# State-space stage: the scan, the segment product and the scaled C are written over the decay tile they are made from, in a pool of three such tiles

## The chip, the cores and the metric

One core of one Trainium2 chip runs the whole kernel as one program. The core's engines work side by side, each with its own stream of instructions: PE (TensorE, matrix products and transposes), DVE (VectorE), ACT (ScalarE), POOL (GpSimd), and SP (SyncE), which here does little but issue DMA transfers. The metric is the device time of one execution in microseconds (us). It was taken in three runs of the kernel before, and once more in an execution recorded by the profiler.

## The reference

A small stack of layers on `x` with 1024 tokens of width 512, all float32:

```python
x = x + 0.5 * _L0_ffn_ref(_layernorm(x), ...)    # 8 experts, mean of the top 2
x = x + _L0_attn_ref(_layernorm(x), ...)         # causal attention, 32 heads
x = x + 0.5 * _L0_ffn_ref(_layernorm(x), ...)    # the same experts again
x = x + 0.5 * _L1_ffn_ref(_layernorm(x), ...)    # dense layer + LoRA experts
x = x + _L1_attn_ref(_layernorm(x), ...)         # state-space layer
x = x + 0.5 * _L1_ffn_ref(_layernorm(x), ...)
```

The change is in the state-space layer. A projection of the normalized `x` gives a gate, an input `x`, a B and a C for each of 8 groups, and a step size `dt` for each of 64 heads; B, C and `x` go through a causal convolution over four tokens and a SiLU. Each group has eight heads of 64 channels with a state of 64 x 128 per head. Then:

```python
dt_p = softplus(dt + dt_bias)
dA = exp(dt_p * -exp(A_log))
dtx = dt_p[..., None] * x
def step(state, inp):
    dA_t, dtx_t, B_t, C_t = inp
    state = state * dA_t[..., None, None] + dtx_t[..., None] * B_t[:, :, None, :]
    y_t = einsum('bhpn,bhn->bhp', state, C_t)
    return state, y_t
y = ys + x * D
yn = y * rsqrt(mean(y * y over the group) + EPS) * norm_weight * silu(gate)
out = einsum('bli,di->bld', yn, out_proj_w)
```

The kernel doesn't step through tokens. For a chunk of 128 tokens and one head, the part of `y` that comes from within the chunk is a product with a 128 x 128 matrix: entry (s, l) is the product of B of token s with C of token l, times the decay from s to l, and 0 where s comes after l. The part that comes from earlier chunks is the state at the chunk's start times C, scaled by the decay from the chunk's start to token l.

## The kernel before, in words

The layers ahead of it (experts, attention, experts, LoRA layer) are not touched. The state-space stage is the function `mamba`. It starts by computing, for all tokens and heads, the step sizes and the decays. The decays of each token (`da`) and those accumulated since the chunk's start (`ecum`) are written to a scratch tensor `decay` in DRAM, in two halves of 512 tokens (the DMA that ends that stretch of code).

Then come 8 groups `g`, each in two halves `hf` of 512 tokens: 16 units of four chunks `i`, 64 chunks in all. In the prediction a chunk is named by its `i` in the unit or by its number 0 to 63. One group of two units needs four weight loads, all from the queue of SP and into a pool of four buffers: `w_bc`, `w_x`, `w_g`, and last `w_out`, which ACT scales (L1044). Each chunk has three parts.

`prepare(un, i)` makes the operands:

- SP issues two DMAs that bring the chunk's decays and accumulated decays of eight heads (1024 floats each) from DRAM, copied to all 128 partitions, into the two halves of a tile `dd` (L1157; 512 KB each).
- DVE runs a scan along the first half, with a unit matrix `eye8` as the addend, and so makes the decays from s to l into a tile `e` (L1163); it then multiplies `e`, in place, with the product `gt` of B and C (L1171).
- PE transposes the convolved `x` (`ps_tr`), DVE multiplies it with the step sizes: `xdt` (L1176). GpSimd makes `xw` of it (L1182) for the next state.
- GpSimd multiplies C with the second half of `dd` into a tile `cs` (L1188; not for the first chunk of a group, which has no state before it).

`scan(un, i, ...)` does the chunk: PE multiplies `xdt` with `e` and the state with `cs`, both into `ps_y` (L1206); DVE adds the skip term (`y_m`, L1215); ACT squares it (`sq`, L1219); DVE multiplies it with the gate (`yg`, L1221); PE makes the chunk's addition to the state (`ps_st`, L1224); GpSimd scales the old state (L1231), DVE adds (L1234); GpSimd sums the squares in two steps (L1236 on 256 columns, L1237 on 128).

`project_out` has PE sum the squares over the partitions (`ps_ss`, L1243), DVE turn that into a normalizing factor `ss` (L149, L150), PE multiply `yg` with `w_out` (`ps_out`, L1250), and DVE scale it and add it to `x` (L1253).

Between these, the next unit's projections are made in slices, two in chunk 0 and one in each of the other three: `ps_in` on PE (L227); the convolution on ACT (L1055) and DVE (L1059, and L1068 for the first columns of a second half, which read the last columns of the first half from `hist`; L1077 writes these); the SiLU on ACT (L1078).

The order in which the program writes this down in chunk `i` is: `scan(i)`, the projection slices for the next unit (at `i == 1` also the transposes and product `gt` of the next unit's B and C), `prepare(i + 1)`, `project_out(i)`. Each engine's own order is then laid down by the framework's scheduler, which keeps to data and buffers: an operation goes no earlier than the buffers it needs can be free.

The tiles named above lie in a pool `m_e` (variable `ep`) of two buffers for each tag: `dd` with 8 KB in each partition, `e` and `cs` with 4 KB each. That makes 32 KB. `m_e` is the last pool opened in the stage.

The last group's units also run the first steps of the LoRA layer that follows (`after.step`), and the last unit has no next unit, so no projections lie between its chunks. The stage runs from about 1850 us of the span nearly to its end.

Of the kernel before, what the change touches and what calls it, by code (L numbers as in the profile page):

```python
# [13 lines left out]
F32 = mybir.dt.float32  # L14
# [8 lines left out]
P = 128  # L23
# [21 lines left out]
HPG = MH // MG  # L45
# [30 lines left out]
def macaron_kernel(  # L76
# [75 lines left out]
    def transposes(src, n):  # L152

        ps = psml.tile([P, 512], F32, tag="ps", name="ps_tr")
        for i in range(n):
            nc.tensor.transpose(ps[:, i * P : (i + 1) * P], src(i), ident)  # L156
        return ps
# [747 lines left out]
    def mamba(lora, par):  # L905
        conv, dsk, nwt, w_dt, dtb, av = par.conv, par.dsk, par.nwt, par.w_dt, par.dtb, par.av
        nct = MI // P
        with ExitStack() as ms:
# [13 lines left out]
            with tc.tile_pool(name="m_dt", bufs=1) as dp, tc.tile_pool(  # L922
                name="m_pair", bufs=3
# [97 lines left out]

            half = S // 2
            w2 = ms.enter_context(tc.tile_pool(name="m_w2", bufs=2))
            ep = ms.enter_context(tc.tile_pool(name="m_e", bufs=2))
            heads = [P, HPG, MP]

            def as_heads(a):
                return a.rearrange("p (h d) -> p h d", d=MP)
# [118 lines left out]
            def per_head(a, un, i):  # L1147
                c, h0 = 4 * un["hf"] + i, un["g"] * HPG
                return a[:, c, h0 : h0 + HPG].unsqueeze(2).to_broadcast(heads)

            def prepare(un, i):

                c, h0 = 4 * un["hf"] + i, un["g"] * HPG
                tok = slice(i * P, (i + 1) * P)
                dd = ep.tile([P, 2, HPG * P], F32, tag="dd", name="dd")
                for q in range(2):
                    nc.sync.dma_start(  # L1157
                        dd[:, q, :],
                        decay[un["hf"]][i, q, h0 * P : (h0 + HPG) * P].partition_broadcast(P),
                    )  # L1160

                e = ep.tile([P, HPG, P], F32, tag="e", name="e_seg")
                nc.vector.tensor_tensor_scan(  # L1163
                    e.rearrange("p h l -> p (h l)"),
                    dd[:, 0, :],
                    eye8.rearrange("p h l -> p (h l)"),
                    0.0,
                    ALU.mult,
                    ALU.add,
                )  # L1170
                nc.vector.tensor_tensor(  # L1171
                    e, e, un["gt"][:, i, :].unsqueeze(1).to_broadcast([P, HPG, P]), ALU.mult
                )
                ps = transposes(lambda k: un["xc"][:, k, tok], 4)
                xdt = w2.tile([P, D], F32, tag="xdt", name="xdt")
                nc.vector.tensor_tensor(  # L1176
                    as_heads(xdt), as_heads(ps), per_head(dtp, un, i), ALU.mult
                )
                xw = None
                if c < NCH - 1:  # L1180
                    xw = w2.tile([P, D], F32, tag="xw", name="xw")
                    nc.gpsimd.tensor_tensor(  # L1182
                        as_heads(xw), as_heads(xdt), per_head(erev, un, i), ALU.mult
                    )
                cs = None
                if c > 0:
                    cs = ep.tile([P, HPG, P], F32, tag="cs", name="cs")
                    nc.gpsimd.tensor_tensor(  # L1188
                        cs,
                        un["cT"][:, tok].unsqueeze(1).to_broadcast([P, HPG, P]),  # L1190
                        dd[:, 1, :].rearrange("p (h l) -> p h l", l=P),
                        ALU.mult,
                    )
                return e, xdt, xw, cs
# [66 lines left out]
            for j in range(5):  # L1261
                project_pair(un, j)
                if j == 1:
                    finish_bc(un)
            ready = prepare(un, 0)
            plan = ((0, 1), (2,), (3,), (4,))
            for n, _ in enumerate(units):
                nxt = None
                if n + 1 < len(units):
                    g, hf = units[n + 1]  # L1270
                    if hf == 0:
                        gr = load_group(g)
                    nxt = begin_unit(gr, hf)
                for i in range(4):
                    done = scan(un, i, *ready)
                    if nxt is not None:
                        for j in plan[i]:
                            project_pair(nxt, j)
                        if i == 1:
                            finish_bc(nxt)  # L1280
                    if i < 3:
                        ready = prepare(un, i + 1)
                    elif nxt is not None:
                        ready = prepare(nxt, 0)
                    project_out(*done)
                    if un["g"] == MG - 1:
                        after.step()
                        if nxt is None:
                            after.step(False)
                        elif i == 3:  # L1290
                            lora.load()
                            lora.store = True
                un = nxt
# [14 lines left out]
    with tc.tile_pool(name="lora", bufs=1) as lp:  # L1308
        lora, par = Lora(lp), Scan(lp)
        expert_ffn("f1", lambda: None, [lora.load, par.ready, par.turn], par.load)  # L1310
        mamba(lora, par)
# [51 lines left out]
```

## Time and profile before

| what | us |
| --- | --- |
| three runs of the kernel before, median | 3008.72 |
| lowest and highest of them | 3002.98, 3010.82 |
| the execution that the profiler recorded | 3011.75 |
| its span, first to last instruction | 3010.0 |

The mean TensorE clock granted over the span was 0.977 of full speed. The busy time of each engine by stretches of the span, in us:

| stretch | what runs | PE | DVE | ACT | POOL | clock |
| --- | --- | --- | --- | --- | --- | --- |
| 0 to 1850 | the layers ahead | 1713.73 | 894.93 | 401.58 | 266.62 | 0.88 to 1.00 |
| 1850 to 1950 | start of the state-space stage | 92.41 | 55.79 | 44.54 | 11.48 | 0.97 |
| 1950 to 2100 | groups | 149.38 | 110.79 | 40.00 | 74.04 | 1.00 |
| 2100 to 2300 | groups | 198.76 | 147.41 | 53.05 | 106.18 | 1.00 |
| 2300 to 2500 | groups | 198.99 | 148.08 | 56.37 | 101.93 | 1.00 |
| 2700 to 2900 | groups | 197.80 | 148.80 | 54.34 | 103.23 | 1.00 |
| 2900 to 3010 | last unit, end of the LoRA layer | 90.43 | 45.82 | 10.99 | 24.64 | 0.91 |

(The first row is the sum of the answers for 0 to 200, 200 to 900 and 900 to 1850 us, with their lowest and highest clock; the stretch from 2500 to 2700 is shown with the prediction.)

How the profile is read: a group of instructions has its engine, its line in the kernel, the operation, `output<-inputs` by the program's names, partitions x elements of output and input, and how often it occurs. Behind these stand the busy time and the mean time of one, then the engine's idle time just before, with what ended most of it ("the releaser"). In a timeline each row begins with its start and its duration in us, and the brackets at its end hold the idle time ahead of it and the releaser. The chain of waits is followed back from the last instruction, at each step to what released it. A busy PE is not PE at its peak, as its instructions' ends are modelled.

### The profile page before, as it was taken

What the parts mean: (1) busy time and instruction counts of PE and PEld (TensorE: products, weight loads), DVE (VectorE), ACT (ScalarE), POOL (GpSimd) and SP (SyncE); (2) the same over time, 40 slices, a digit from 0 to 9 for tenths busy, and PEclk for the clock granted to TensorE, in tenths of its full rate; (3) what the DMA queues carried; (4) which work ended last, traced back from release to release, by engine and by line L of the source; (5) the groups of instructions that cost most, each with busy time, mean ns of one, the idle gap of its engine ahead of it and who ended that gap; (6) DMA issues with size and microseconds to landing.
All of it is one profiled execution on the core that took longest, in us unless ns stands there. A gap on an engine that the chain in (4) does not pass through costs nothing.

```text
span 3010.0 us, 29285 instructions
## 1 busy us (share of the span) xinstructions
PE 2840.7 (94%) x10691; PEld 1525.9 (51%) x10691; DVE 1692.8 (56%) x3183; ACT 711.7 (24%) x1381; POOL 791.1 (26%) x601
## 2 busy tenths in 40 slices
PE   5979999999999999999999787999999999999988
PEld 3435646456564565655655344455555555455544
DVE  3146545465454654546445315677776777777673
ACT  1212212122121321213122121523222232222310
POOL 3231002020020200202000222144545545555451
PEclk8989999999999999999999898999999999999999
DMA  8420001010010100100002441232322322323210
GB/s 283 126 74 29 14 15 35 8 42 14 14 42 3 40 15 14 42 15 28 15 14 86 171 121 50 87 95 81 103 96 91 112 77 99 105 84 117 86 43 28
DMA packets 102174, 196.94 MB, mean 65 GB/s; under 512 B 9040, under 2 KB 34800, under 8 KB 102032
## 3 DMA queue, kind: packets, MB, share of 16 engines
q1 hardware_dynamic: 84896, 157.15, 15.8%
q0 software_dynamic: 6240, 20.45, 2.7%
q10 hardware_dynamic: 10896, 17.47, 1.6%
q8 instruction: 87, 1.43, 0.2%
q14 instruction: 55, 0.45, 0.1%
HBM read 176.17 MB, written 18.87 MB: 65 GB/s over the span
## 4 chain that ended last, share of the span: by engine, by line
PE 78%; DVE 12%; POOL 4%; issue 3%; DMA 2%; ACT 1%; POOLq 0%; DVEq 0%; SPq 0%; ACTq 0%
PE ps_in L227 14%; PE ps_m L823 13%; PE ps_o L728 8%; PE ps_wo L763 7%; PE ps_tr L156 6%; PE ps_out L1250 6%; PE ps_m L797 6%; PE ps_e L506 5%; PE ps_s L704 4%; DVE nm L715 3%; PE ps_y L1206 3%; PE ps_up L238 2%; DVE pr L720 1%; PE ps_st L1224 1%; DVE xc L1059 1%
## 5 line engine op out<-in xcount | busy, mean ns | idle before, releaser
L704 PE MATMUL ps_s<-kT,qT 128*128 128x512 f32 (+3 forms) x768 | 293.0, 491 | 1.8
L749 ACT COPY pT<-ps_tr 128x256 f32<-128x256 f32 (+2 forms) x192 | 91.9, 479 | 820.1 <-PE ps_tr L156 817.5
L728 PE MATMUL ps_o<-pT,v 128*128 128x512 f32 (+3 forms) x768 | 260.7, 489 | 0.0
L1250 PE MATMUL ps_out<-w_out,yg 128*128 128x512 f32 x512 | 240.7, 614 | 0.0
L227 PE MATMUL ps_in<-hT,w_g 128*128 128x512 f32 x512 | 227.1, 596 | 7.3 <-issue 7.3
L1188 POOL TENSOR_TENSOR cs<-cT,dd 128x1024 f32<-128x1024 f32 x56 | 183.5, 3278 | 162.6 <-PE ps_y L1206 140.4
L227 PE MATMUL ps_in<-hT,w_x 128*128 128x512 f32 x512 | 225.8, 593 | 0.0
L763 PE MATMUL ps_wo<-w_o,oT 128*128 128x512 f32 x512 | 222.0, 592 | 0.0
L718 ACT ACTIVATE pr<-ps_s,nm 128x128 f32<-128x128 f32 (+7 forms) x256 | 190.3, 743 | 132.5 <-DVE nm L715 107.8
L728 PEld LDWEIGHTS ps_o<-pT,v 128*128 128x128 f32 x768 | 146.4, 191 | 143.7 <-issue 107.2
L156 PE MATMUL ps_tr<-ident,pr 128*128 128x128 f32 x1152 | 172.9, 277 | 31.2 <-DVE sm L719 22.9
L632 POOL TENSOR_TENSOR sv<-w_v 128x512 f32<-128x512 f32 x7 | 8.9, 1269 | 723.3 <-PE ps_tr L156 466.9
L156 PEld LDWEIGHTS ps_tr<-ident,pr 128*128 128x128 f32 x1152 | 134.6, 142 | 115.3 <-issue 52.9
L715 DVE TENSOR_REDUCE nm<-ps_s 128x1 f32<-128x128 f32 (+7 forms) x256 | 189.4, 750 | 2.2
L506 PE MATMUL ps_e<-w_all,xt_s 128*128 (+1 forms) x368 | 168.8, 603 | 0.0
L227 PEld LDWEIGHTS ps_in<-hT,w_g 128*128 128x128 f32 x512 | 96.6, 190 | 126.9 <-issue 126.9
L227 PEld LDWEIGHTS ps_in<-hT,w_x 128*128 128x128 f32 x512 | 97.0, 190 | 121.0 <-issue 120.6
L1163 DVE TENSOR_TENSOR_SCAN e_seg<-dd,eye 128x1024 f32<-128x1024 f32 x64 | 152.3, 2380 | 7.8 <-PE ps_y L1206 6.8
L704 PEld LDWEIGHTS ps_s<-kT,qT 128*128 128x128 f32 x768 | 127.9, 193 | 54.8 <-issue 33.7
L763 PEld LDWEIGHTS ps_wo<-w_o,oT 128*128 128x128 f32 x512 | 96.2, 190 | 115.8 <-issue 115.8
L1059 DVE SCALAR_TENSOR_TENSOR xc<-ps_in,conv,xc 128x511 f32<-128x511 f32 (+2 forms) x192 | 141.6, 738 | 17.8 <-ACT xc L1055 17.4
L720 DVE TENSOR_SCALAR pr<-pr,sm 128x128 f32<-128x128 f32 (+7 forms) x256 | 145.8, 570 | 4.5
(252 smaller groups left out, 4416.8 us busy)
## 6 DMA issues: line engine op xcount, KB each, us to landing
dd<-decay SPq DMA_DIRECT2D x128, 512.0 KB
w_all<-in_w_e_dram SPq DMA_DIRECT2D x16, 1024.0 KB
outs<-y_e ACTq DMA_DIRECT2D x46, 256.0 KB
w_v<-in_wkv_dram SPq DMA_DIRECT2D x8, 1024.0 KB
w_q<-in_wq_dram SPq DMA_DIRECT2D x32, 256.0 KB
w_k<-in_wkv_dram SPq DMA_DIRECT2D x8, 1024.0 KB
w_o<-in_wo_dram SPq DMA_DIRECT2D x8, 1024.0 KB
w_x<-in_in_wt_dram SPq DMA_DIRECT2D x8, 1024.0 KB
```

Of the source, the lines that this page charges most:

```text
L156: nc.tensor.transpose(ps[:, i * P : (i + 1) * P], src(i), ident)
L227: nc.tensor.matmul(ps[:, cols : cols + n], lhsT=w[:, k, c0 : c0 + P], rhs=hT[:, k, t0 : t0 + n], start=(k == 0), stop=(k == KT - 1),)
L506: nc.tensor.matmul(ps, lhsT=xt[:, k, :], rhs=w_all[:, bass.ds(ep, 1), k, :].rearrange("p e c -> p (e c)"), start=(k == 0), stop=(k == KT - 1),
L704: nc.tensor.matmul(ps[:, j : j + m], lhsT=qT[:, qt * P : (qt + 1) * P], rhs=kT[:, j : j + m], start=True, stop=True,)
L715: nc.vector.tensor_reduce(nm, ps[:, :n], AX.X, ALU.max, negate=True)
L718: nc.scalar.activation(pr[:, :n], ps[:, :n], AF.Exp, bias=nm, accum_out=sm)
L728: nc.tensor.matmul(ps[:, lo:512], lhsT=v[:, kb, hh * P : (hh + 1) * P], rhs=pT[:, kb, lo:512], start=(kb == 0), stop=(kb == last),)
L763: nc.tensor.matmul(ps, lhsT=heads[hh][:, t * P : (t + 1) * P], rhs=w[:, hh, :], start=(hh == 0), stop=(hh == HG - 1),)
L797: nc.tensor.matmul(ps[:, t * 256 : (t + 1) * 256], lhsT=right[i][:, k, (j + t) * P : (j + t + 1) * P], rhs=left_v[i][:, k, :], start=(firs ...
L823: nc.tensor.matmul(ps, lhsT=gr["left"][i][:, k, hh * P : (hh + 1) * P], rhs=right[i][:, k, :], start=(first and k == 0), stop=(last and k ...
L1188: nc.gpsimd.tensor_tensor(cs, un["cT"][:, tok].unsqueeze(1).to_broadcast([P, HPG, P]), dd[:, 1, :].rearrange("p (h l) -> p h l", l=P), ALU ...
L1250: nc.tensor.matmul(po, lhsT=yg[:, k, :], rhs=w_o[:, k, :], start=(k == 0), stop=(k == 3))
```

## The change

The pool `m_e` gets three buffers instead of two, and only `dd` is left in it: 3 x 8 KB are 24 KB in each partition, where 2 x (8 + 4 + 4) were 32. The scan now writes `e` over the half of `dd` that it reads; the product with `gt` was in place on `e` before, and so is over `dd` as well. GpSimd writes `cs` over the other half of `dd`. No instruction is added or taken away, and no shape changes but for the way in which the tile is indexed. A tile `dd` is thus in use from its load until PE has read `e` and `cs` for `ps_y`.

```diff
--- before.py
+++ after.py
@@ -1021,7 +1021,7 @@
 
             half = S // 2
             w2 = ms.enter_context(tc.tile_pool(name="m_w2", bufs=2))
-            ep = ms.enter_context(tc.tile_pool(name="m_e", bufs=2))
+            ep = ms.enter_context(tc.tile_pool(name="m_e", bufs=3))
             heads = [P, HPG, MP]
 
             def as_heads(a):
@@ -1152,17 +1152,17 @@
 
                 c, h0 = 4 * un["hf"] + i, un["g"] * HPG
                 tok = slice(i * P, (i + 1) * P)
-                dd = ep.tile([P, 2, HPG * P], F32, tag="dd", name="dd")
+                dd = ep.tile([P, 2, HPG, P], F32, tag="dd", name="dd")
                 for q in range(2):
                     nc.sync.dma_start(
-                        dd[:, q, :],
+                        dd[:, q, :, :].rearrange("p h l -> p (h l)"),
                         decay[un["hf"]][i, q, h0 * P : (h0 + HPG) * P].partition_broadcast(P),
                     )
 
-                e = ep.tile([P, HPG, P], F32, tag="e", name="e_seg")
+                e = dd[:, 0, :, :]
                 nc.vector.tensor_tensor_scan(
                     e.rearrange("p h l -> p (h l)"),
-                    dd[:, 0, :],
+                    e.rearrange("p h l -> p (h l)"),
                     eye8.rearrange("p h l -> p (h l)"),
                     0.0,
                     ALU.mult,
@@ -1184,11 +1184,11 @@
                     )
                 cs = None
                 if c > 0:
-                    cs = ep.tile([P, HPG, P], F32, tag="cs", name="cs")
+                    cs = dd[:, 1, :, :]
                     nc.gpsimd.tensor_tensor(
                         cs,
                         un["cT"][:, tok].unsqueeze(1).to_broadcast([P, HPG, P]),
-                        dd[:, 1, :].rearrange("p (h l) -> p h l", l=P),
+                        cs,
                         ALU.mult,
                     )
                 return e, xdt, xw, cs
```

## Predicted, before the changed kernel was run

> **What bounds the kernel now.** I read the page's busy shares first, then busy time by stretches, then the chain of waits, and last the timeline of one group. The change touches the state-space stage alone, and there TensorE is full:
>
> ```profile
> PE 2840.7 (94%) x10691; PEld 1525.9 (51%) x10691; DVE 1692.8 (56%) x3183; ACT 711.7 (24%) x1381; POOL 791.1 (26%) x601
> 2500.00:2700.00 200.00, 199.14 (x887) 103.06 (x886) 141.21 (x187) 50.83 (x74) 103.02 (x72) 1.00 0.28 92
> ```
>
> The second line gives busy us of PE, PEld, DVE, ACT, POOL in 200 us of the stage, then granted clock, DMA share and GB/s: PE idles 0.9 of 200 us at full clock. So nothing can be gained there beyond a few us. But the chain that ended last leaves PE once in every group of eight chunks (period 127.14 us, eight groups) and runs over VectorE and GpSimd, where a group begins (chunks i=0 to 2 of its first half). VectorE is nearly without a pause there, and PE waits for it by fractions of a us. In the group at 2456 (start, duration, engine, line, operation, and in brackets the idle time before it):
>
> ```profile
> 2456.62 0.38 SPq L145 DMA_DIRECT2D w_out<-in_out_wt_dram  x1
> 2462.34 2.56 ACT L1044 ACTIVATE w_out<-w_out,nwt 128x512 f32<-128x512 f32 x4 [3.25 <-DMA w_out<-in_out_wt_dram]
> 2466.33 0.75 DVE L1059 SCALAR_TENSOR_TENSOR bT<-ps_in,conv,bT 128x511 f32<-128x511 f32 x1 [2.97 <-ACT bT L1055]
> 2478.43 2.35 POOL L1188 TENSOR_TENSOR cs<-cT,dd 128x1024 f32<-128x1024 f32 x1 [1.51 <-PE ps_y L1206]
> 2479.07 1.74 DVE L1068 SCALAR_TENSOR_TENSOR xc<-hist,conv,xc 128x2 f32<-128x2 f32 x1
> 2488.41 0.38 PE L1243 MATMUL ps_ss<-ones,sq 128*128 128x1 f32 x2 [0.38 <-POOL sq L1237]
> 2502.83 0.38 PE L1243 MATMUL ps_ss<-ones,sq 128*128 128x1 f32 x2 [0.24 <-POOL sq L1237]
> ```
>
> See three things: the w_out load occupies the queue until 2462.3; VectorE has 2.97 us of slack before it starts the convolution of bT; PE's wait for the squares is 0.38 and 0.24 us, so delay past that slack reaches PE.
>
> **The change, part by part.** PE's and ACT's streams keep their order; VectorE, GpSimd and SP change.
>
> *Buffers.* Before, a decay tile dd was free once the scan and cs of its chunk had read it, and was reloaded for chunk i+2; e and cs, two each, were held until ps_y. Now one of three tiles is held from its load to ps_y, and is reloaded for chunk i+3 after ps_y(i). GpSimd's wait for a cs buffer (140.4 us in total in the list of waits) goes, but it was slack of an engine that is off the path: worth nothing by itself. In-place work I cost at 0: the segment product is in place already (1.21 us), and GpSimd's in-place sq takes 0.46 us at 128 columns and 0.72 at 256, 2.0 ns a column, no more than cs out of place (2350/1024 = 2.3). An in-place scan has no row; it might be dearer, not cheaper, by at most a few tenths.
>
> *The order on VectorE.* After y_m(i) now come the scan and mostly the product of chunk i+3, ahead of the convolutions and of xdt(i+1). Before, the scan of chunk i+2 stood there and its data had landed long before. Now the load starts at the end of ps_y(i). From the trace's landing events, a pair of dd transfers issued at 2420.20 has its first half in at 2423.8 (3.6 us) and its second at 2425.5 (5.3). The scan needs the first half, cs the second. In an ordinary chunk VectorE has y_m, yg and the state to do (2 us), then waits 1.5; scan and product end 7.3 us after ps_y, or 9.3 if cs comes between; xdt is due at about 12. Those chunks cost nothing.
>
> *Chunk i=0 of groups 1 to 7.* Here the dd load is queued behind w_out, whose last bytes land at 2462.26; the dd half behind it landed at 2464.26 although it was issued only at 2460.65. Issued at 2457.6 it lands hardly sooner, 2464.1 (2.0 us behind w_out). VectorE is free at 2459.6 and waits 4.5 us. Scan 2464.1 to 2466.4. By then cs has its data and starts, and the product stands behind it.
>
> What that costs turns on the port between the two engines. Row first: cs takes 2.35 us alone; beside a scan of 2.29 us (2444.55 to 2446.84), it began at 2445.47 and took 3.53, ending 2.16 after the scan. The 128x2 operation of L1068 takes 0.2 us, but 1.74 (shown above) where it began within cs and ended with it. The Trainium skill (SBUF — State Buffer, "SBUF: two separate sides") says that VectorE with two SBUF inputs and GpSimd lock the shared pair for a whole instruction, and the other blocks. By average rows the product would end 1.5 us after the scan (its median of 1570 ns); by the rule and these rows it waits out cs: 2466.4 + 2.2 + 1.1 = 2469.7. I take the latter.
>
> So bT starts at 2469.7, 3.4 late. cT waits for ACT behind bT and follows; xdt comes at 2475.2 instead of 2472.8, just in time for ps_y at 2476.4; ACT's xc comes 3 us later, and so do the convolution and x+=. The cs that stood in i=1 is gone, with its 1.5 us block of L1068: y_m(1) at 2483.3 instead of 2481.5. Then state, yg, GpSimd's next-state product (which locks the scan out for 1 us), scan to 2488.6, the squares at 2489.8. **PE's ps_ss at 2489.9 instead of 2488.4: +1.5.** cs, now behind the squares, blocks a hist operation until 2492; gt and xdt(2) end at 2494.3, where PE needs them at 2493.8: **+0.6.** In i=2, y_m(2) is at 2499.7 (before 2497.6), level with the PE that is 2.1 late; but scan and product now stand behind it and alternate on the port with sq, state and sq: 0.65 + 2.25 + 1.0 + 1.1 + 0.5 after 2501.5 gives 2507.0, so ps_ss is at 2507.1 instead of 2502.8, **+2.2** more. Sum 4.3 us a group, seven groups: **+30.1.** Group 0 has no w_out in front: 0. Bounds: if the pauses of VectorE (0.72 and 0.88 before cT and xdt) absorb their full 1.6 and i=2 costs nothing, 1.2 a group (+8); if the product and cs meet in i=1 as well, 6 a group (+42). I take 4.3, from rows one by one.
>
> *The prologue.* Three dd pairs are now requested at once, and a third scan stands on VectorE before the conversions that free a PSUM buffer for PE:
>
> ```profile
> 1927.17 0.15 DVE L1077 COPY hist<-ps_in 128x3 f32<-128x3 f32 x1
> 1927.42 2.05 PE L227 MATMUL ps_in<-hT,w_g 128*128 128x512 f32 x2 [7.35 <-issue]
> ```
>
> PE starts when hist ends. One scan more is 2.28 us: **+2.3**, nothing covers it. The second decay write is issued behind six dd loads instead of eight, long before it is ready: 0. All later weight loads on SP keep their place in time, since each dd load that waits for ps_y(i) replaces one that waited for a scan shortly after it.
>
> *The tail.* In the last unit no projections cover the chain, and there scan and cs stood ahead of y_m and the squares:
>
> ```profile
> 2914.01 0.59 PE L1243 MATMUL ps_ss<-ones,sq 128*128 128x1 f32 x2 [5.15 <-POOL sq L1237]
> 2914.46 5.80 PE L1250 MATMUL ps_out<-w_out,yg 128*128 128x512 f32 x8
> 2935.00 0.38 PE L1243 MATMUL ps_ss<-ones,sq 128*128 128x1 f32 x2 [4.12 <-POOL sq L1237]
> 2953.39 0.38 PE L1243 MATMUL ps_ss<-ones,sq 128*128 128x1 f32 x2 [1.44 <-POOL sq L1237]
> 2953.63 3.68 PE L1250 MATMUL ps_out<-w_out,yg 128*128 128x512 f32 x8
> ```
>
> The last pair is chunk 62, with no scan and no cs: what chunks 60 and 61 become. Waits 5.15 and 4.12 become 1.44: -3.7 and -2.7. After the long waits ps_out ran slow (5.80, and 5.38 in chunk 61) against 3.68: -2.1 and -1.7. The skill (TensorE: Matmul & The Clock Gate, Part 1) has the clock halved after an idle window of about 3.4 us; by it only the two waits over 3.4 cost clock, but in chunk 63 a wait of 2.92 is followed by a ps_out of 5.09. The row decides: waits must fall to about 1.5, which they do. Against this: chunk 63's scan and product, behind its cs, now precede x+= of chunk 60: +2.5; in chunk 59 cs locks out the normalization before the product and xdt: +1.7. **-6.0**, between -10 and 0.
>
> **Sum.** The profiled execution took 3011.75 us (span 3010.0 and 1.75 around it): 2.3 + 30.1 - 6.0 = +26.4, 3038.2. The median of the runs is 3.0 lower: **3035.**
>
> **Rivals.** (1) *Faster.* The load waits find enough slack on VectorE, and only the removed waits count: tail -10.2, ps_ss waits in the groups -0.6 times 8, prologue +2.3: 3008.7 - 12.7 = 2996. For it: PE holds the stage and VectorE is 26 to 30% idle; against: it is not idle where a group begins. (2) *No net change.* The low bound of the groups, +8, with the prologue and a tail of -10: 3009. For it: the pauses named. (3) *Much slower*, one mechanism: dd lands too late in every chunk. That decides once the first half needs over 6 us instead of 3.6, as when several transfers are queued; at 1.5 us for each of 56 chunks, +84, 3093. Against: at 28% DMA share a pair meets no queue except behind w_out. That the change doesn't do what it says: the 8 KB serve nothing else, since this pool is the last one opened.
>
> **Chances.** Forecast 0.62, (1) 0.14, (2) 0.16, (3) 0.08. About 0.3%, 9 us, is what can be told from no change. Faster 0.13; same 0.17; slower 0.70. The forecast's own range, from the bounds of group and tail, is 3018 to 3048; to leave out no more than 2 in 10 it reaches down to 3004 and up to 3050.
>
> **What would show it.** Period of a group 131 instead of 127.1 us, first group excepted; VectorE idle before the scan for a dd transfer, about 4.5 us where w_out loads; PE's wait for sq in i=1 and i=2 near 2 us each; PE's pause at 1920 grown to 9.6; waits near 1.5 in chunks 60 and 61. A period still at 127 would make it wrong, and so would a dd first half that lands under 5 us after ps_y beside w_out.

## The result and the profile after

The changed kernel took 3021.17 us (median of 8 runs, 3015.82 to 3023.26), the kernel before 3011.81 us in 8 runs beside it; ratio 1.0028, 95% interval 1.0019 to 1.0038. So it is slower, by some 8.4 us, where 26 had been forecast. Its profiled execution spans 3020.3 us, 10.3 more than before.

Busy time by engine of the changed kernel, and the groups of the three instructions that now write in place (busy us, mean ns of one, idle time ahead); below them the scans of the kernel before.

```profile
PE 2838.1 (94%) x10691; PEld 1526.4 (51%) x10691; DVE 1726.2 (57%) x3183; ACT 711.9 (24%) x1381; POOL 713.6 (24%) x601
...
L1163 DVE TENSOR_TENSOR_SCAN dd<-dd,eye 128x1024 f32<-128x1024 f32 x64 | 162.8, 2543 | 75.9 <-DMA dd<-decay 75.8
...
L1188 POOL TENSOR_TENSOR dd<-cT,dd 128x1024 f32<-128x1024 f32 x56 | 154.2, 2754 | 98.6 <-DMA dd<-decay 79.1
...
L1171 DVE TENSOR_TENSOR dd<-dd,gt 128x1024 f32<-128x1024 f32 x64 | 156.2, 2442 | 1.5
```

```profile
L1163 DVE TENSOR_TENSOR_SCAN e_seg<-dd,eye 128x1024 f32<-128x1024 f32 x64 | 152.3, 2380 | 7.8 <-PE ps_y L1206 6.8
```

VectorE idles 75.9 us ahead of the scans, and nearly all of it is a wait for the dd transfer; before, those 64 scans had 7.8 us. How little of it reaches PE shows in the same stretch of the span as before (PE, PEld, DVE, ACT, POOL busy, clock, DMA share, GB/s):

```profile
2500.00:2700.00 200.00, 195.39 (x874) 101.25 (x872) 150.26 (x193) 51.81 (x76) 87.89 (x70) 1.00 0.27 90
```

PE idles 4.6 of 200 us instead of 0.9. Measured between the starts of each chunk's ps_ss, the two traces differ as follows (us; the first column holds the terms of the prediction):

| part | forecast | measured |
| --- | --- | --- |
| layers ahead of the stage | 0 | +2.1 |
| prologue, first projection to ps_ss of chunk 0 | +2.3 | +2.2 |
| group 0 | 0 | +0.8 |
| groups 1 to 6 | 6 x 4.3 = +25.8 | +2.5, +1.3, +2.0, +1.8, +1.9, +2.2: +11.7 |
| group 7 up to chunk 58 | +4.3 | +0.1 |
| tail, from ps_ss of chunk 58 | -6.0 | +1.5 - 8.2 + 0.1 = -6.6 |
| sum | +26.4 | +10.3 |

The first row is not the change: nothing differs there between the kernels, and in the other profiled executions below the stage began between 6.4 us earlier and 1.4 later than before. The error lies in the groups. Inside a group (mean of groups 1 to 6, delay against before, counted from ps_y of i=0): ps_ss of i=1 **+0.1**, forecast 1.5; ps_y of i=2 **+0.7**, forecast 2.1; ps_ss of i=2 **+1.9**, forecast 4.3.

The timeline of the changed kernel in the group of the prediction, 10.8 us later than there (start, duration, brackets: idle time before). First i=0:

```profile
2467.44 0.38 SPq L145 DMA_DIRECT2D w_out<-in_out_wt_dram  x1
...
2468.43 1.63 SPq L1157 DMA_DIRECT2D dd<-decay  x2
...
2474.54 2.29 DVE L1163 TENSOR_TENSOR_SCAN dd<-dd,eye 128x1024 f32<-128x1024 f32 x1 [3.49 <-DMA dd<-decay]
...
2475.87 3.12 POOL L1188 TENSOR_TENSOR dd<-cT,dd 128x1024 f32<-128x1024 f32 x1 [3.15 <-issue]
...
2476.87 3.20 DVE L1171 TENSOR_TENSOR dd<-dd,gt 128x1024 f32<-128x1024 f32 x1
...
2479.99 0.74 DVE L1059 SCALAR_TENSOR_TENSOR bT<-ps_in,conv,bT 128x511 f32<-128x511 f32 x1
```

All of this is of the kind that was forecast: the dd load behind w_out, VectorE idle for it, the product that waits out the scaled C (3.20 us, ending 1.08 after it, where a product alone takes 1.21), and bT late, by 2.8 us where 3.4 had been forecast. The chain starts late, and then it catches up. At i=1 and i=2:

```profile
2498.76 0.49 POOL L1237 TENSOR_TENSOR sq<-sq 128x128 f32<-128x128 f32 x1
...
2499.21 2.34 POOL L1188 TENSOR_TENSOR dd<-cT,dd 128x1024 f32<-128x1024 f32 x1
...
2499.30 0.38 PE L1243 MATMUL ps_ss<-ones,sq 128*128 128x1 f32 x2 [0.44 <-POOL sq L1237]
...
2499.51 2.06 DVE L1068 SCALAR_TENSOR_TENSOR xc<-hist,conv,xc 128x2 f32<-128x2 f32 x1
...
2503.61 1.09 PE L1206 MATMUL ps_y<-dd,xdt 128*64 128x128 f32 x16 [0.38 <-DVE xdt L1176]
...
2510.06 0.98 POOL L1236 TENSOR_TENSOR sq<-sq 128x256 f32<-128x256 f32 x1 [2.18 <-ACT sq L1219]
...
2510.37 2.81 DVE L1163 TENSOR_TENSOR_SCAN dd<-dd,eye 128x1024 f32<-128x1024 f32 x1
...
2511.00 3.02 POOL L1231 TENSOR_TENSOR state<-state,etot 128x512 f32<-128x512 f32 x1
...
2513.98 1.43 POOL L1237 TENSOR_TENSOR sq<-sq 128x128 f32<-128x128 f32 x1
...
2515.47 0.38 PE L1243 MATMUL ps_ss<-ones,sq 128*128 128x1 f32 x2 [1.53 <-POOL sq L1237]
```

The kernel before at i=2:

```profile
2499.20 1.18 POOL L1236 TENSOR_TENSOR sq<-sq 128x256 f32<-128x256 f32 x1
...
2499.72 1.74 DVE L1171 TENSOR_TENSOR e_seg<-e_seg,gt 128x1024 f32<-128x1024 f32 x1
...
2500.34 2.02 POOL L1231 TENSOR_TENSOR state<-state,etot 128x512 f32<-128x512 f32 x1
...
2502.33 0.45 POOL L1237 TENSOR_TENSOR sq<-sq 128x128 f32<-128x128 f32 x1
```

See PE's three waits: 0.44 for the squares at i=1 (before: 0.38), 0.38 for xdt, and 1.53 for the squares at i=2 (before: 0.24). GpSimd's state product for the next chunk stands between the two sums of squares of i=2 in both kernels. Before, only a product ran on VectorE beside it. Now the scan stands there, which before had run ahead of y_m. It shuts the state product out (3.02 us; 1.04 alone), and the product behind the scan then holds up the second sum (1.43 instead of 0.45). From the start of y_m to the end of the second sum, i=2 takes 6.8 us where it took 5.2. At i=1 it's the other way round, 6.0 instead of 6.8: the scan there is now for the next unit, whose gt doesn't exist yet, so no product follows it and the second sum takes 0.49 us instead of 1.32. The i=2 wait is 1.5 us in each of groups 0 to 6; the i=1 wait is 0.0, 1.1, 0.0, 0.6, 0.4, 0.0, 0.9.

### The profile page after: what moved, and what is told of

It is laid out like the page before. It is cut to its first block, busy times and chain, and to the rows that moved or that the text cites. A ratio compares the mean times of both kernels' runs of the same rounds, so it can differ in the third digit from the quotient of the medians.

```text
span 3020.3 us, 29266 instructions
## 1 busy us (share of the span) xinstructions
PE 2838.1 (94%) x10691; PEld 1526.4 (51%) x10691; DVE 1726.2 (57%) x3183; ACT 711.9 (24%) x1381; POOL 713.6 (24%) x601
## 3 DMA queue, kind: packets, MB, share of 16 engines
q8 instruction: 87, 1.43, 0.2%
## 4 chain that ended last, share of the span: by engine, by line
PE 76%; DVE 14%; POOL 4%; DMA 3%; issue 2%; ACT 1%; SPq 0%; POOLq 0%; DVEq 0%; ACTq 0%
PE ps_m L823 13%; PE ps_in L227 12%; PE ps_o L728 8%; PE ps_wo L763 7%; PE ps_out L1250 6%; PE ps_tr L156 6%; PE ps_m L797 6%; PE ps_e L506 5%; PE ps_s L704 4%; DVE nm L715 3%; PE ps_y L1206 3%; PE ps_up L238 2%; DVE pr L720 1%; DVE xc L1059 1%; PE ps_st L1224 1%
## 5 line engine op out<-in xcount | busy, mean ns | idle before, releaser
L1163 DVE TENSOR_TENSOR_SCAN dd<-dd,eye 128x1024 f32<-128x1024 f32 x64 | 162.8, 2543 | 75.9 <-DMA dd<-decay 75.8
L1188 POOL TENSOR_TENSOR dd<-cT,dd 128x1024 f32<-128x1024 f32 x56 | 154.2, 2754 | 98.6 <-DMA dd<-decay 79.1
L1171 DVE TENSOR_TENSOR dd<-dd,gt 128x1024 f32<-128x1024 f32 x64 | 156.2, 2442 | 1.5
```

## The experiments

Theory A said: the loss of a group is an order on the port that VectorE and GpSimd share, with scan and product of chunk i+3 beside the sums of squares of i=2. A2 added: what differs between groups is the dd load behind a weight load. Rivals: B, the late load alone; C, in-place instructions are slower; D, the moved scaled C; others are named where they come. "Tail" below is the time from ps_ss of chunk 59 to that of chunk 63: 73.4 us before, 65.2 in the changed kernel. Of each edit the main lines are shown.

**Two tiles instead of three (e1).** One number of the changed kernel:

```diff
-            ep = ms.enter_context(tc.tile_pool(name="m_e", bufs=3))
+            ep = ms.enter_context(tc.tile_pool(name="m_e", bufs=2))
```

> The changed kernel with two dd tiles instead of three (16 KB), all else in place. Theory A (the loss in the groups is order: the third tile puts scan and product of chunk i+3 between the two sums of squares of i=2): GpSimd's order at i=2 is now both sums before the state product, so PE's wait for sq there falls from 1.5 to under 0.4 us, a group takes 127.2 to 128.0 us, the prologue loses its +2.2 (74.0), the tail loses its gain (73 to 75): 3013 to 3019 in all. Rival B (the loss is the late load: dd is freed by ps_y and lands 3.6 to 5.3 us later): groups stay at 129 us, as the load is just as late here, and the time is 3024 or more, since the tail gain is gone. Rival C (in-place instructions are slower): groups stay at 129.

Measured: 1.0014 of before (1.0007 to 1.0020). The i=2 wait went to 0.0 in all groups, as A says. But groups 1 to 6 still lost 1.8 us in the mean (128.0 to 130.0), as B says: now their i=1 wait was 0.5 to 2.1, as the product follows the scan there again and the second sum takes 1.32 us. The tail was 65.6, its gain kept; both A and B had it lost. So neither holds as it was put, and the tail's gain does not come from the third tile: a load that waits for ps_y drives scan and scaled C behind the squares with two tiles as well.

**The scaled C alone in place (e2), the scan alone in place (e3).** Each keeps three dd tiles and gives the other result two tiles of its own (32 KB):

```diff
+            ep2 = ms.enter_context(tc.tile_pool(name="m_e2", bufs=2))
...
-                e = dd[:, 0, :, :]
+                e = ep2.tile([P, HPG, P], F32, tag="e", name="e_seg")
...
```

```diff
+            ep2 = ms.enter_context(tc.tile_pool(name="m_e2", bufs=2))
...
-                    cs = dd[:, 1, :, :]
+                    cs = ep2.tile([P, HPG, P], F32, tag="cs", name="cs")
...
```

> Three dd tiles, the scaled C in place, the scan and product out of place in two e tiles (32 KB). VectorE's order is that of before; loads are a whole chunk early. Theory A: waits of i=1 and i=2 are those of before (0.4, 0.2), groups 127.1 to 127.4, prologue 74.0, tail near 73: 3010 to 3014. Rival B agrees (no late load). Rival C would have GpSimd's cs take longer than the 2.35 us that it took alone before.

> Three dd tiles with the scan and product in place, the scaled C out of place in two tiles (32 KB). VectorE's order is that of the changed kernel, GpSimd's that of before. Theory A: i=2 wait 1.5 us again, groups 128.5 to 129.5, prologue +2.2, tail between 65 and 70 as cs stands ahead of the squares there again: 3020 to 3027. Rival D (the moved cs is what costs): groups back to 127.1.

e2: 0.9999 of before (0.9991 to 1.0008), groups 127.2, waits 0.0 and 0.6. Its prologue was 76.1, though no third scan is there: a third scaled C on GpSimd now locks VectorE instead (the small L947 takes 2.32 us there, before 0.29). Its tail was 69.7. e3: 0.9990 of before (0.9983 to 0.9997), groups 127.3. That was forecast by D, not by A: VectorE's order and its late dd are those of the changed kernel, and nearly the whole loss is gone. Two rows of e3 at i=0 (lines of code one further down), and one at i=1 behind the scan:

```profile
2465.35 2.29 DVE L1164 TENSOR_TENSOR_SCAN dd<-dd,eye 128x1024 f32<-128x1024 f32 x1 [4.24 <-DMA dd<-decay]
2467.68 1.23 DVE L1172 TENSOR_TENSOR dd<-dd,gt 128x1024 f32<-128x1024 f32 x1
...
2489.92 0.20 DVE L1069 SCALAR_TENSOR_TENSOR xc<-hist,conv,xc 128x2 f32<-128x2 f32 x1
```

At i=0 the load is late by 4.24 us, more than in the changed kernel here, and the product takes 1.23 instead of 3.20: the scaled C waits for ps_y of its own chunk and is not there. But that gain does not last. The scaled C comes at i=1 ahead of y_m instead and blocks VectorE there, so that y_m of i=1 starts 25.8 us after ps_y of i=0, in the changed kernel 25.9. What e3 wins lies behind that: in the changed kernel the scaled C follows the squares of i=1 and blocks the small L1068 for 2.06 us, in e3 the same instruction takes 0.20, and y_m of i=2 starts 39.3 us after ps_y of i=0 instead of 41.3. With that start the state product may be shut out at i=2 just as long (3.02 us), and PE waits 0.4 to 1.0 us.

Rival C falls by these traces: the in-place scan takes 2.29, as out of place before (2.28 and 2.29), the in-place product 1.21 to 1.23 (before: 1.21), and the in-place C 2.34 (before: 2.35).

**The state updated in place (e4), and the same on the kernel before (e6).** GpSimd's state product then has to wait for ps_y of its own chunk, and so leaves the place between the sums:

```diff
-                    st = w2.tile([P, D], F32, tag="state", name="state")
+                    st = before
                     if before is None:
+                        st = w2.tile([P, D], F32, tag="state", name="state")
                         nc.vector.tensor_copy(st, pst)
```

> The changed kernel, and the state is updated in place, so that GpSimd's state product waits for ps_y of its own chunk and stands ahead of the sums of squares at every chunk instead of between the two at i=2; nothing else moves. Theory A: the i=2 wait of 1.5 us falls to 0.5 or less, groups 1.0 to 1.5 us shorter (127.5 to 128), prologue and tail as in the changed kernel: 3011 to 3015. Rival B: the i=2 wait stays at 1.5, 3020 to 3023.

> The kernel before with the state updated in place, nothing else. It tells how much of the gain of the same edit on the changed kernel belongs to the edit alone. Theory A: the two waits of a group (0.38 and 0.24 us) fall to between 0 and 0.3 us, groups 126.5 to 127.1, prologue and tail as before, so 0 to 5 us are gained: 3006 to 3011. Rival F (the edit is worth the 18 us everywhere): 2993.

e4: 0.9969 of before (0.9956 to 0.9981), median 3001.17; the i=2 wait is 0.0 in all groups, groups 126.0 to 127.1. GpSimd at i=2 in e4:

```profile
2495.59 1.04 POOL L1232 TENSOR_TENSOR state<-state,etot 128x512 f32<-128x512 f32 x1
2497.80 0.98 POOL L1237 TENSOR_TENSOR sq<-sq 128x256 f32<-128x256 f32 x1 [1.17 <-ACT sq L1219]
2498.86 2.32 POOL L1238 TENSOR_TENSOR sq<-sq 128x128 f32<-128x128 f32 x1
```

First to last sum of squares is 3.4 us (2497.80 to 2501.18), in the changed kernel 5.35. One lock by the scan remains, but nothing is queued behind it ahead of the second sum. e6: 0.9990 of before (0.9980 to 0.9999), 126.5 a group: the same edit is worth 0.6 us a group on the kernel before and 2.3 on the changed one. From y_m to the end of the sums, i=1 gets shorter by it in both (before 6.8 to 6.0 us, changed 6.0 to 5.1), i=2 only in the changed kernel (6.8 to 4.9; before 5.2 with and without). So most of what the two gains differ by is the i=2 loss.

**w_out elsewhere (e5), and w_out once (e9).** e5 gives w_out of every second group a buffer of its own; e9 loads and scales w_out for group 0 alone and uses these rows for all groups, so what it computes is not the layer.

```diff
-                gr["w_o"] = w_o = weights(out_wt[g * 512 : (g + 1) * 512, :], "w_out")
+                w_o = (wop if g % 2 else wpool).tile([P, KT, D], F32, tag="w", name="w_out")
+                gr["w_o"] = w_o
...
```

```diff
+                if g == 0:
+                    w_o = only["w_o"] = wop.tile([P, KT, D], F32, tag="w", name="w_out")
...
+                gr["w_o"] = only["w_o"]
```

> The changed kernel, with w_out of every second group in a buffer of its own (8 KB), so that its load goes out half a group or more earlier and half of the groups have no w_out load in front of the dd load of their first chunk. Theory A2 (the i=1 part of the loss, wait of 0 to 1.1 us and xdt of i=2 late by 0.5, comes from the dd that lands behind w_out; the i=2 wait of 1.5 is the order and does not care): in the groups without it VectorE's idle time before that scan falls from about 3.5 to 1.5 us, the i=1 wait is 0 and the group takes 128.0 or less, as group 0 of the changed kernel (127.96); the others stay at 128.5 to 129.5; i=2 waits stay at 1.5 in all. Time 3016 to 3020. Rival E (w_out has no part): all groups stay spread between 128.4 and 129.6.

> The changed kernel with w_out loaded and scaled for group 0 alone and used for all eight groups (it leaves out seven loads and scalings of w_out, and projects groups 1 to 7 with the rows of group 0), so that no weight load stands ahead of the dd load of a group's first chunk. Theory A2 (what differs between groups, i=1 wait 0 to 1.1 us, is the load ahead of dd): the scan of i=0 starts 3.5 to 3.9 us after ps_y in every group, as in group 0, where it was 5.5 to 6.8; the i=1 waits are 0 and ps_y of i=2 is not late; the i=2 wait of 1.5 stays; every group takes 127.9 to 128.1. Rival E: groups still spread from 128.4 to 129.6.

e5 told nothing about its question: 1.0033 of before (1.0023 to 1.0044). The buffer that ps_out frees at a group's start went to w_bc of the next group, and where w_out was gone w_bc stood ahead of dd instead; in these groups that scan still came 5.5 to 6.3 us after ps_y. In e9 no weight load stands ahead of dd. Scan after ps_y: 3.8 to 4.5 us in every group; i=1 waits 0.0 in all; ps_y of i=2 0.5 early instead of 0.7 late; i=2 wait still 1.2 to 1.5; groups 127.5 to 128.0. At i=0 of e9 (lines four further down):

```profile
2466.61 2.29 DVE L1167 TENSOR_TENSOR_SCAN dd<-dd,eye 128x1024 f32<-128x1024 f32 x1 [1.87 <-DMA dd<-decay]
2468.93 3.19 DVE L1175 TENSOR_TENSOR dd<-dd,gt 128x1024 f32<-128x1024 f32 x1
```

The product is locked out as in the changed kernel (3.19), but VectorE's wait for the load is 1.6 us shorter. So A2 holds: 1.2 of the 1.9 us of a group are the load behind a weight load. e9 also leaves out ACT's scaling of w_out. In the group shown that is no rival: in the changed kernel ACT is done with it at 2475.90 and then idles 0.45 us until PE has made the projection for bT. (Its 1.0000 of before, 0.9991 to 1.0008, is no gain, as work is left out.)

**One tile held through the prologue (e7).** A dd tile is taken, one column of it is set, and it is given back after gt of the first unit:

```diff
+            held = ep.tile([P, 2, HPG, P], F32, tag="dd", name="held")
+            nc.vector.memset(held[:, 0, 0, 0:1], 0.0)
...
+            nc.vector.tensor_copy(held[:, 0, 0, 1:2], un["gt"][:, 0, 0:1])
             ready = prepare(un, 0)
```

> The changed kernel, with one of its three dd tiles taken until gt of the first unit is written, so that only two scans and two scaled C can go ahead of the conversions in the prologue. Theory A: prologue back from 76.2 to 73.5 to 74.2 us, groups and tail as in the changed kernel: 3018 to 3020. Rival G (the third tile has no part in the prologue's +2.2): 76.2 stays.

Measured: 1.0010 of before (0.9999 to 1.0021); prologue 71.8, below the 74.0 of before, as also the second scaled C no longer locks VectorE there (the small L945 takes 0.28 us, before 1.78). PE's pause ahead of the w_g projection, in the changed kernel and then in e7:

```profile
1932.06 2.05 PE L227 MATMUL ps_in<-hT,w_g 128*128 128x512 f32 x2 [9.90 <-issue]
```

```profile
1927.42 2.05 PE L227 MATMUL ps_in<-hT,w_g 128*128 128x512 f32 x2 [5.95 <-issue]
```

**The edits together (e8, e10, e11).** e8 is e4, e5 and e7 in one; e10 is e4 and e7; e11 is e10 with the scaled C out of place as in e3.

> The changed kernel with all three edits: state in place, one tile held through the prologue, w_out of every second group in a buffer of its own. If the parts add: the time with the state in place alone, 3001.2, less 2.5 for the prologue and 0 to 2 for the groups: 2997 to 2999, groups near 126.0 to 126.6. If the i=1 delay is slack there already, the w_out edit gives nothing: 2999.

> The changed kernel with state in place and one tile held through the prologue, w_out as it was. If w_out's place gave nothing in the run with all three edits, groups are 126.0 to 127.1 again, prologue 73.5, and the time is that of the run with all three, 0.9968 of before (0.996 to 0.9975).

> As the run with state in place and one tile held, and the scaled C out of place in two tiles (32 KB). If the scaled C ahead of the product at i=0 and the state product between the sums are two separate delays of one path, taking both away gives little over one, since PE is near its floor: groups 126.0 to 126.5 without spread, tail 67 (2 us longer, cs ahead of the squares there): 0.9955 to 0.997 of before.

e8: 0.9968 (0.9962 to 0.9975), e10: 0.9954 (0.9941 to 0.9967), e11: 0.9957 (0.9944 to 0.9969) of before. The w_out edit gives nothing in e8, but it doesn't take the weight load away there either: in its groups the scan of i=0 comes 5.6 to 6.6 us after ps_y. That the late load is nearly slack once the state product is out of the way shows in e4 and e10 themselves, whose i=1 waits are at most 0.28 and 0.35 us. e11 has the shortest groups (126.4 in the mean, all but one 126.3) and gives that back in the tail (70.1, where 67 had been expected; e10: 65.2). e10 and e11 cannot be told apart; both are faster than both kernels of this study, e10 with the 24 KB of the changed one.

| kernel | groups 1 to 6, mean against before | i=1 wait | i=2 wait |
| --- | --- | --- | --- |
| changed | +1.9 | 0 to 1.1 | 1.5 |
| e1 two tiles | +1.8 | 0.5 to 2.1 | 0.0 |
| e9 no load ahead of dd | +0.7 | 0.0 | 1.2 to 1.5 |
| e3 scaled C out of place | +0.2 | 0 to 0.3 | 0.4 to 1.0 |
| e2 scan out of place | 0.0 | 0.0 | 0.6 |
| e4 state product out of the way | -0.4 | 0 to 0.3 | 0.0 |
| e6 before, state the same | -0.6 | 0.0 | 0.2 |

Three things make up the loss: the late load, the scaled C at its new places, and scan and product beside the sums of i=2. The parts do not add: against the changed kernel, e3 is worth 1.8 us a group, e4 2.3, and both together in e11 2.7. They lie on one path, and what comes earlier than PE needs it is lost. Taking away one of the last two is enough to bring the group back to 127.3 or less.

## Why the prediction was right and wrong

**What bounds it, and the direction: right.** PE holds the stage, a group begins with a chain over VectorE and GpSimd, and delay past a few tenths reaches PE. The time went up.

**The prologue: right.** +2.3 forecast, +2.2 measured; the third scan stands on VectorE ahead of hist, and e7 takes away more than it cost. e2 adds what the step left out: a third scaled C costs as much as a third scan.

**The lock between product and scaled C: right.** By the rule of whole instructions the product was to end 3.3 us after the scan at i=0, by average rows 1.5; it ended 3.2 after it (2476.83 to 2480.07).

**The groups: the mechanism right, the size wrong by a factor of more than two.** The step that failed is "PE's ps_ss at 2489.9 instead of 2488.4: +1.5": it was +0.1 in the mean. Followed through the group shown, with 10.8 us taken off: the first half of dd landed 0.4 us sooner than forecast (the scan began at 2463.7, not 2464.1); bT began at 2469.2 instead of 2469.7; y_m at 2482.4 instead of 2483.3, helped by a small L1068 that takes 0.21 us where it took 0.56 beside GpSimd's xw; and the squares were done 6.0 us after y_m, at 2488.5, instead of 6.5, as the scan ended 4.9 us after y_m, just as in before (2481.51 to 2486.43), where the forecast had 5.3. These are errors of 0.1 to 0.4 us, all to the same side, where the whole forecast lay 1.5 us over the slack. The bounds of that step were set too narrow: "1.2 a group" was the lowest value, and only when the pauses took 1.6 and i=2 cost nothing; e9's groups show that the i=1 part alone moves by 1.2 with the landing of one load.

The next step, "+0.6" for ps_y of i=2, was right. "+2.2 more" for ps_ss of i=2 was too much: it was 1.3. The queue of locks was as forecast (scan, state product, second sum), but y_m stood nearly at its old place (2497.8, before 2497.6; forecast 2499.7). And two groups were put on the wrong side. Group 0 was counted at 0 for having no w_out ahead, though the i=2 order does not depend on it: +0.8 there. Group 7 was counted like the others: in both traces its waits at i=1 and i=2 are 0.0 to 0.05, in the last group, where steps of the next layer lie between PE's work. The trace of before has these rows, and the forecast did not use them; that it is those steps that cover was not tested.

**The tail: the sum near, in part by luck.** Forecast -6.0, measured -6.6. The changed kernel's PE in the tail:

```profile
2929.12 0.38 PE L1243 MATMUL ps_ss<-ones,sq 128*128 128x1 f32 x2 [1.91 <-POOL sq L1237]
2929.37 5.38 PE L1250 MATMUL ps_out<-w_out,yg 128*128 128x512 f32 x8
2946.88 0.38 PE L1243 MATMUL ps_ss<-ones,sq 128*128 128x1 f32 x2 [1.36 <-POOL sq L1237]
2947.12 3.68 PE L1250 MATMUL ps_out<-w_out,yg 128*128 128x512 f32 x8
```

The waits fell from 5.15 and 4.12 to 1.91 and 1.36 (forecast 1.44 each), and ps_out of chunk 61 is quick again, that of chunk 60 is not: -0.4 instead of -2.1. Against it, the +2.5 for chunk 63's scan ahead of chunk 60's x+= did not show; chunk 59's +1.7 did, as +1.5. So two terms were wrong, to opposite sides. A quick ps_out of chunk 60 would not have helped: in e7 and e9 it takes 3.68 us after the same wait, and PE then waits 3.69 us for VectorE's zm (a step of the next layer) instead of 2.00.

**The range and the rivals.** The range 3018 to 3048 does not come out of the forecast's own bounds: 1.2 to 6 us a group and a tail of -10 to 0 give 3009 to 3053. *Faster* fell with the measured +8.4. *Much slower* (every chunk late) fell too: the load is awaited in every chunk, 75.9 us in all, and ordinary chunks cover it, as argued. *No net change*, from groups at +1.2, was nearer than the forecast at 4.3: groups 1 to 6 were at +1.9, groups 0 and 7 at +0.8 and +0.1.

## What to carry to other kernels

Work written over its input ties the input's buffer to the last reader of the result, and so moves the next load, and with it everything that the scheduler orders by that load: look at what is then side by side on engines that share a port, not at the bytes saved. A delay on an engine with slack costs what is left over after each pause behind it; add such steps up from one chain with its waits, and test the sum at the group that lacks the cause (here group 0) and at the one that differs (the last). When an experiment brings the time back, follow the gain along the chain to where it is kept: in e3 the lock at i=0 that went away was not the one that counted. And where one short GpSimd operation decides PE's start, see what is queued in front of it: moving the state product away gave more than all the changed kernel lost.

## What the hardware showed beyond that

PE's slow ps_out after a wait has no sharp edge in these runs. In the last eight chunks of the thirteen profiled kernels, after waits for the squares up to 1.63 us it took 3.68 us each time; after 3.19 to 6.26 us it took 5.06 to 6.37; between, both happen: after 1.90 to 1.92 us three times 3.68 and once 5.38, after 2.67 and 2.68 once 3.68 and once 5.30, after 2.92 twelve times 5.09 to 6.66 and once 3.68. The clock granted from 2930 to 2947 us in the changed kernel, behind the wait of 1.91, was 0.81, and 1.00 in the 17 us after it. The slow phase can also fall on other matmuls. e4 and e8 have equal waits at chunk 60 (1.63 and 1.62 us for the squares, then 2.63 for zm), and yet from its ps_ss to that of chunk 61 pass 18.1 us in e4 and 15.1 in e8: behind zm the two halves of ps_y took 1.98 and 1.67 us in e4, 1.09 and 1.04 in e8, and the clock from 2905 to 2925 us was 0.83 and 1.00. So the tails of two runs can differ by 3 us with equal waits. A wait of 1.91 us is also shorter than the idle window of about 3.4 us that the Trainium skill gives (TensorE: Matmul & The Clock Gate, Part 1).
